# A graph layer on one core: where a sum waits for its second load of edges, and the order of two loads and two copies

## The chip, the core and the metric

The kernel runs on one core of a Trainium2 chip. The core has a matrix engine (PE, with PEld for the loading of its weights), three elementwise engines (DVE, ACT, POOL), an engine that mostly issues transfers (SP), and 16 DMA engines that carry the transfers which SP, ACT and POOL ask for. Each engine works through its own list of instructions in order and waits on semaphores for the others. The metric is the time of one execution on the device in microseconds (us); lower is better.

## The reference

A graph has 12500 nodes with 128 numbers each and 412500 edges with 48 numbers each; the edges are sorted by their target node `dst`. What is computed, cut to the core:

```python
h   = maximum(layernorm(x), 0)                     # 12500 x 128
agg = segment_sum(edge_attr_48, dst, 12500)        # 12500 x 48, the sum of a node's edges
u   = graph_globals[0]                             # the same 64 numbers for every node
hid = relu(concat([h, agg, u]) @ W1 + b1)          # 12500 x 256
out = x + hid @ W2 + b2                            # 12500 x 128
```

All numbers are fp32. `src` isn't used in the result.

## The kernel before

**Tiles.** The work goes in 12 rounds of 1024 nodes and a rest of 212. A round's nodes are two halves, A and B, of 512 (tiles `xa`, `xb`). A round has 11 groups of edges of 3072 each (576 KB), which lie in six slots (`SLOTS`): slots 0 to 3 hold two groups each, slot 4 one, slot 5 two. Each group has a load of its own: `le0.0` and `le0.1` are the first and the second load of slot 0. Eleven loads of the next round are asked for while a round runs, each as soon as the sum that read the slot is done.

**The sum of a slot.** DVE compares each edge's place with a row of 28 numbers, which gives a one-hot tile (`oh`, line 676). PE multiplies these with the edges (`add_up`, line 695): 24 products for each group, so 48 for a slot of two groups, and the first 24 read the first load alone, the last 24 the second alone. An fp32 product stands in the trace as two matmul records and two weight loads, so a slot of two groups is 96 records. The sums of the slots are called `su0` to `su5` below. They go by turns to two banks of PSUM, and ACT copies each to SBUF (`ss`, line 699), which frees the bank for the sum after the next. PE then places the sums of each group at their nodes by a second one-hot product (`place`, line 717, into `ax` and `ay`), and ACT copies these to `ags` (`sums_out`, line 760).

**The nodes.** DVE takes mean and variance of `xa` and `xb` (`stats`, line 724), ACT scales them (`norm`, line 745), PE turns them (`turn`, line 754), and the two layers follow (lines 764 and 769 into four banks, relu on ACT in line 774, line 790 for the second layer). POOL adds the bias to the old x (`xba`, `xbb`, line 749), after which ACT may ask for the next x into the same tiles.

**The order.** The class `Flow` records every operation with what it reads and writes, in the order in which `prologue`, `body` and `epilogue` are written, and works out which semaphores each must wait for. Each engine runs its operations in that order. An operation with several waits has one of them on its first instruction; the others go ahead of it as instructions of their own that only wait (`emit`, line 174; such an instruction can hold two waits). PE's loop is turned: one pass of it begins with `su3` of a round and ends with `su0`, `su1`, `su2`, the first placings and the second layer of the next one. On PE the order within a round is: `su0`, `su1`, `su2`, placings, line 790 for A and B, `su3`, `su4`, `su5`, turning of A and B, placings, lines 764 and 769.

**The lines that matter here.** Line 70 (`op`) and line 174 (`emit`): where waits are put. Line 691 (`add_up`): the operation whose waits are split. Lines 807 to 813 (`prologue`): SP's list of first loads, in which the first x stands behind slot 1's edges. Lines 924 to 933 (`body`): ACT's list at the end of a round: the copies of the turned x (line 755), the asking for the next x, the copies `ags`.

Of the kernel before, what the change touches and what calls it, by code (L numbers as in the profile page):

```python
# [20 lines left out]
T = 6  # L21
CE = P * T
CG = 4
# [3 lines left out]
IN = 1024  # L27
BN = 512
# [26 lines left out]
class Flow:  # L55
# [11 lines left out]
        self.seq = []  # L67
        self.at = None

    def op(self, eng, name, reads, writes, emit, dma=False):  # L70
        self.seq.append(dict(eng=eng, name=name, r=tuple(reads), w=tuple(writes), emit=emit, dma=dma, it=self.at))

    def chain(self, eng, name, reads, writes, *fns):

# [98 lines left out]

    def emit(self, o, waits, i):
        eng = self.of[o["eng"]]
        for s, v in waits[1:]:
            eng.wait_ge(s, v)
        made = o["emit"](i)
        if waits:
            made[0]._wait_ge(*waits[0])  # L180
        if o["name"] in self.sem:
            made[-1].then_inc(self.sem[o["name"]], self.unit(o["name"]))

# [2 lines left out]

    def straight(self, some):
        for o in some:
            self.emit(o, [(self.sem[d["name"]], self.value(d)) for d in o["waits"]], o["it"])

    def run(self):


        lo, hi = self.loop
        nc = self.nc
        start = [o for o in self.seq if o["it"] is None or o["it"] < lo]
        body = [o for o in self.seq if o["it"] == lo]
        end = [o for o in self.seq if o["it"] is not None and o["it"] > hi]
        for e in self.of:
            self.prepare(e)  # L200
        self.straight([o for o in start if o["eng"] != "PE"])
        regs = {}
        for o in body:
            for n, back in self.body.get(o["name"], []):
                u = self.unit(n)
                key = (o["eng"], u, (self.at_lo[n] - lo - back + self.extra[n]) * u)
                if key not in regs:
                    r = self.of[o["eng"]].alloc_register(f"w_{o['eng']}_{len(regs)}")
                    self.of[o["eng"]].reg_mov(r, key[2] + lo * u)
                    regs[key] = r  # L210

        def ahead(e):
            for n, c in sorted(self.ahead[e].items()):
                self.of[e].wait_ge(self.sem[n], (self.rank[n, c] + self.extra[n]) * self.unit(n))

        def repeat(o, i):
            waits = []
            for n, back in self.body.get(o["name"], []):
                u = self.unit(n)
                waits.append((self.sem[n], regs[(o["eng"], u, (self.at_lo[n] - lo - back + self.extra[n]) * u)]))  # L220
            self.emit(o, waits, i)

        def count(e):
            for (f, u, _), r in regs.items():
                if e == f:
                    self.of[e].reg_add(r, r, u)

        others = [e for e in self.of if e != "PE"]
        for e in others:
            ahead(e)  # L230
        every = {o["name"] for o in self.seq if o["it"] == hi}
        with nc.Fori(lo, hi + 1, 1, engines=[self.of[e].engine for e in others]) as i:
            for e in others:
                mine = [o for o in body if o["eng"] == e]
                for always, some in groupby(mine, lambda o: o["name"] in every):
                    with ExitStack() as last:
                        if not always:
                            last.enter_context(self.of[e].If(i < hi))
                        for o in some:
                            repeat(o, i)  # L240
            for e in others:
                count(e)
        own = [o for o in body if o["eng"] == "PE"]
        cut = [o["name"] for o in own].index(self.mark)
        with nc.Fori(0, hi - lo + 2, 1, engines=[nc.tensor.engine]) as j:
            with nc.tensor.If(j > 0):
                for o in own[cut:]:
                    repeat(o, None)
                count("PE")
            with nc.tensor.If(j < 1):  # L250
                self.straight([o for o in start if o["eng"] == "PE"])
                ahead("PE")
            with nc.tensor.If(j < hi - lo + 1):
                for brief, some in groupby(own[:cut], lambda o: o["name"] in self.brief):
                    some = list(some)
                    if not brief:
                        for o in some:
                            repeat(o, None)
                        continue
                    with nc.tensor.If(j < 1):  # L260
                        for o in some:
                            repeat(dict(o, emit=self.brief[o["name"]]), None)
                    with nc.tensor.If(j > 0):
                        for o in some:
                            repeat(o, None)
        self.straight(end)
# [151 lines left out]
def kernel(  # L418
# [18 lines left out]
    NIT = E // IE  # L437
# [61 lines left out]
    u = const.tile([G, 1], F32)  # L499
# [23 lines left out]
    f = Flow(nc, tc)  # L523
    op = f.op
    A, B, Z = 0, 1, 2
# [37 lines left out]
    def rows_of(ap, i, a, m, r):  # L563
        return span(ap, i, a, m * r).rearrange("(p r) d -> p (r d)", r=r)

    def load_x(k, a, m=P, eng="ACT"):
        r = RR[k]
        dv = xt[k].rearrange("p r d -> p (r d)")
        q = m - m % 16
        dma(eng, f"lx{k}", [], [f"x{k}"], dv[:q], lambda i: rows_of(x, i, a, q, r))  # L570
        if q < m:
            dma(eng, f"lx{k}t", [], [f"x{k}t"], dv[q:m], lambda i: rows_of(x, i, lambda i: a(i) + q * r, m - q, r))
# [118 lines left out]
    def add_up(name, k, o, ev, sv, reads, n):  # L691

        m = -(-n // CG)
        op("PE", f"su{name}", [f"oh{name}"] + reads, [f"S{k}"], lambda i: [
            nc.tensor.matmul(  # L695
                S[k][NV * c:NV * c + V, j * DE:(j + 1) * DE], o[:, (j * CG + c) * T + t], ev[:, j * CG + c, t * DE:(t + 1) * DE],
                start=(t == 0), stop=(t == T - 1), skip_group_check=True)
            for j in range(m) for t in range(T) for c in range(min(CG, n - j * CG))])
        op("ACT", f"ss{name}", [f"S{k}"], [f"ss{name}"], lambda i: [nc.scalar.copy(sv.rearrange("p j d -> p (j d)"), S[k][:, :m * DE])])  # L699

    def sums(s):
        m = len(SLOTS[s])
        add_up(s, s % 2, oh[s], e[s], ss[s], [f"e{s}.{j}" for j in range(m)], m * CG)
# [53 lines left out]
    def sums_out(k, m=P):  # L757
        h, r = HI * (k % 2), RR[k]
        op("ACT", f"ag{k}", [f"bk{k % 2}"], [f"ag{k}"], lambda i: [
            nc.scalar.copy(ag[k // 2][h:h + DE, :, :m], agg[k % 2][h:h + DE, :m * r].rearrange("p (c r) -> p r c", r=r))])  # L760
# [41 lines left out]
    def prologue():  # L802
# [2 lines left out]
            load_dst(b)  # L805
        dma("SP", "le5.1", [], ["e5.1"], e[5][:, CG:], edge_attr[:GE].rearrange("(c p t) d -> p c (t d)", p=P, t=T))
        for s in range(NS):
            if s == 2:
                load_x(A, lambda i: 0, eng="SP")
                load_x(B, lambda i: BN, eng="SP")  # L810
            for k in (0, 1):
                if (s, k) != (5, 1) and k < len(SLOTS[s]):
                    load_e(s, 1, k)
# [71 lines left out]
    def body(it):  # L885
        f.at = it

        def add_slots(*some):
            for s in some:
                sums(s)  # L890
                if it < NIT - 1:
                    load_e(s, 1)

        keep = lambda i: (i + NIT - 2) % (NIT - 1)
        farthest()
        fetch(1)
        add_slots(0, 1)
        for k in (A, B):
            stats(k)
            variance(k)  # L900
        add_slots(2)
        onehots(0)
        shift(A)
        shift(B)
        onehots(1)
        onehots(2)
        norm(A)
        norm(B)
        place(5, (0,), 0)
        place(0, (1,))  # L910
        place(1)
        places(5)
        fetch_off(1)
        places(0)
        places(1)
        for k in (A, B):
            second(k, P, ph[k], f"PH{k}", keep)
        for k in (A, B):
            add_b(k)

        add_slots(3, 4, 5)
        for s in (3, 4, 5):
            onehots(s)
        turn(A)
        turn(B, P, po, "PO")
        if it < NIT - 1:
            load_x(A, lambda i: (i + 1) % NIT * IN)
            load_x(B, lambda i: (i + 1) % NIT * IN + BN)
        for s in (2, 3, 4):
            place(s)  # L930
        place(5, (), 1)
        sums_out(A)
        sums_out(B)
        for s in (2, 3, 4):
            places(s)
        layers(layer_x)
        layers(layer_e)
        layers(relu)
# [91 lines left out]
```

## Time and profile before

| what | value |
|---|---|
| time, median of 3 runs (lowest, highest) | 268.95 us (268.59, 269.54) |
| the profiled execution's own time | 268.61 us |
| its span in the profile | 266.8 us |
| PE busy, share of the span | 246.5 us, 92% |
| DVE busy | 240.3 us, 90% |
| ACT busy | 126.3 us, 47% |
| POOL busy | 54.3 us, 20% |
| moved by DMA, mean rate | 94.33 MB, 354 GB/s |

A share of the span is a mean over a first round, which starts from nothing, eleven rounds that follow it, and a rest. The view of waits tells which engine stood still and for whom; the chain of work that ended last tells which engine set the end at each moment; the timeline gives single groups of instructions with their start (us from the span's start), their length and the idle time ahead of them. A matmul's end is modelled: a row's length holds the last record's own length, about 0.2 us, besides the steps from record to record.

### The profile page before, as it was taken

How to read it: one execution, taken by the hardware profiler on the slowest of the kernel's cores; microseconds unless marked ns; L12 is line 12 of the kernel's file. 1: busy time of each engine (PE TensorE's matmuls, PEld its weight loads, DVE VectorE, ACT ScalarE, POOL GpSimd, SP SyncE). 2: the span in 40 equal slices, each digit the busy share in tenths (PEclk: the TensorE clock that was granted, in tenths of full speed). 3: DMA queues.
4: the chain of work that ended last, by engine and by line, in shares of the span. 5: the costliest groups of instructions: out<-in, count | busy, mean ns of one | idle time of the engine just before them, and what ended most of it. 6: DMA issues, size and time to landing. Idle time of an engine off the chain costs nothing.

```text
span 266.8 us, 17173 instructions
## 1 busy us (share of the span) xinstructions
PE 246.5 (92%) x7539; PEld 191.9 (72%) x7540; DVE 240.3 (90%) x593; ACT 126.3 (47%) x314; POOL 54.3 (20%) x47
## 2 busy tenths in 40 slices
PE   0874899999999999999999999999999999999990
PEld 0864766967958949949859769679589498598580
DVE  6699999999999999989999989989899999899441
ACT  4630526545537438246445455364374373464420
POOL 8100050050140410500500501403204105007000
PEclk9975799999999999999999999999999999999999
DMA  6999999999999999999999999999999999979911
GB/s 201 289 385 383 364 391 392 390 393 390 390 393 387 390 393 371 390 392 344 391 385 350 391 345 372 393 357 378 393 343 389 394 334 390 393 232 379 377 68 63
DMA packets 79012, 94.33 MB, mean 354 GB/s; under 512 B 3227, under 2 KB 72189, under 8 KB 78998
## 3 DMA queue, kind: packets, MB, share of 16 engines
q1 hardware_dynamic: 75398, 87.63, 93.1%
q10 hardware_dynamic: 3312, 6.03, 5.9%
q0 software_dynamic: 288, 0.49, 0.7%
q8 instruction: 7, 0.11, 0.2%
q14 instruction: 7, 0.06, 0.1%
HBM read 87.75 MB, written 6.40 MB: 353 GB/s over the span
## 4 chain that ended last, share of the span: by engine, by line
PE 86%; DVE 6%; issue 2%; DMA 1%; ACT 1%; SPq 0%; DVEq 0%
PE s L695 26%; PE ph L790 17%; PE ph L764 9%; PE ax L717 7%; PE ph L769 5%; PE pt L764 4%; PE po L764 4%; PE pt L769 4%; PE ay L717 3%; DVE oh L676 3%; PE pt L754 3%; PE po L754 2%; DMA holda<-in_dst_dram 1%; DVE pl L682 1%; PE s L952 1%
## 5 line engine op out<-in xcount | busy, mean ns | idle before, releaser
L676 DVE TENSOR_TENSOR oh<-iota_v,rel_i 128x1344 f32<-128x1344 f32 (+1 forms) x78 | 130.7, 1715 | 0.0
L695 PEld LDWEIGHTS s<-e,oh 128*28 128x28 f32 x6336 | 74.7, 109 | 17.6 <-issue 14.8
L695 PE MATMUL s<-e,oh 128*28 128x48 f32 x6336 | 79.4, 210 | 6.6 <-issue 3.2
L749 POOL TENSOR_TENSOR xba<-xa,b_sb 128x512 f32<-128x512 f32 x12 | 15.5, 1288 | 191.0 <-DVE holda L794 191.0
L699 ACT COPY ss<-s 128x96 f32<-128x96 f32 (+1 forms) x72 | 16.8, 235 | 60.0 <-PE s L695 60.0
L682 DVE TENSOR_SCALAR pl<-iota_w,off_i 128x186 f32<-128x186 f32 x141 | 35.0, 307 | 0.5
L749 POOL TENSOR_TENSOR xbb<-xb,b_sb 128x512 f32<-128x512 f32 x12 | 31.1, 2592 | 0.0
L717 PE MATMUL ax<-pl,ss 128*48 128x186 f32 (+3 forms) x172 | 26.9, 298 | 0.0
L717 PE MATMUL ay<-pl,ss 128*48 128x186 f32 (+3 forms) x168 | 26.1, 296 | 0.0
L774 ACT ACTIVATE hida<-ph,bias 128x512 f32<-128x512 f32 x12 | 8.2, 687 | 35.1 <-PE ph L769 35.1
L790 PE MATMUL ph<-w,hida 128*128 128x128 f32 x192 | 24.6, 281 | 0.0
L790 PEld LDWEIGHTS ph<-w,hida 128*128 128x128 f32 x192 | 22.3, 191 | 3.2 <-issue 3.1
L790 PE MATMUL ph<-w,hidb 128*128 128x128 f32 x192 | 23.4, 275 | 0.0
L790 PEld LDWEIGHTS ph<-w,hidb 128*128 128x128 f32 x192 | 22.4, 192 | 0.0
L745 ACT ACTIVATE xna<-xa,sha,sca 128x128 f32<-128x128 f32 x48 | 19.8, 483 | 3.8 <-DVE sha L741 3.6
L717 PEld LDWEIGHTS ax<-pl,ss 128*48 128x48 f32 x172 | 17.6, 126 | 4.3 <-issue 2.0
L745 ACT ACTIVATE xnb<-xb,shb,scb 128x128 f32<-128x128 f32 x48 | 19.6, 480 | 0.0
L717 PEld LDWEIGHTS ay<-pl,ss 128*48 128x48 f32 x168 | 17.8, 124 | 0.0
L769 PE MATMUL ph<-ags,w1a 48*128 48x512 f32 x48 | 14.1, 641 | 0.0
L724 DVE BATCH_NORM_STATS2 sta<-xa 128x6 f32<-128x128 f32 x48 | 10.4, 280 | 3.8 <-DMA xa<-in_x_dram 3.7
L760 ACT COPY ags<-ax 48x512 f32<-48x512 f32 x12 | 7.0, 579 | 14.3 <-POOL xbb L749 13.4
L764 PE MATMUL ph<-hta,w1h 128*128 128x512 f32 x24 | 13.5, 645 | 0.0
(155 smaller groups left out, 305.8 us busy)
## 6 DMA issues: line engine op xcount, KB each, us to landing
e<-in_edge_attr_dram SPq DMA_DIRECT2D x133, 576.0 KB, 8.6
xa<-in_x_dram ACTq DMA_DIRECT2D x11, 256.0 KB, 5.4
xb<-in_x_dram ACTq DMA_DIRECT2D x11, 256.0 KB, 5.6
out_dram<-holda SPq DMA_DIRECT2D x11, 256.0 KB, 3.5
out_dram<-holdb SPq DMA_DIRECT2D x11, 256.0 KB, 3.5
holda<-in_dst_dram SPq DMA_DIRECT2D x4, 384.0 KB, 5.1
e<-in_edge_attr_dram SPq DMA_DIRECT2D x1, 720.0 KB, 4.3
xa<-in_x_dram SPq DMA_DIRECT2D x1, 256.0 KB, 10.0
```

Source lines behind the costliest of these rows:

```text
L676: op("DVE", f"oh{name}", reads + ["iota_v"], [f"oh{name}"], lambda i: [nc.vector.tensor_tensor(ov, iota_v[:, None, None, :].to_broadcast([ ...
L682: nc.vector.tensor_scalar(out[:, j], iota_w, o[j], None, OP.is_equal) for j in range(len(o))])
L695: nc.tensor.matmul(S[k][NV * c:NV * c + V, j * DE:(j + 1) * DE], o[:, (j * CG + c) * T + t], ev[:, j * CG + c, t * DE:(t + 1) * DE], start ...
L699: op("ACT", f"ss{name}", [f"S{k}"], [f"ss{name}"], lambda i: [nc.scalar.copy(sv.rearrange("p j d -> p (j d)"), S[k][:, :m * DE])])
L717: out.append(nc.tensor.matmul(agg[bk][h:h + DE, at:at + w], sv[:, j], pv[:, j, frm:frm + w], start=bk in fresh and bk not in seen, stop=Tr ...
L724: op("DVE", f"st{k}", [f"x{k}", f"x{k}t"], [f"st{k}"], lambda i: [nc.vector.bn_stats(st[k][:m, r], xt[k][:m, r]) for r in range(RR[k])])
L745: nc.scalar.activation(xn[k][:m, r], xt[k][:m, r], AF.Relu, bias=sh[k][:m, r:r + 1], scale=sc[k][:m, r:r + 1]) for r in range(RR[k])])
L749: nc.gpsimd.tensor_tensor(xb[k][:m], xt[k][:m], b2_sb[:m, None, :].to_broadcast([m, RR[k], D]), OP.add)])
L754: op("PE", f"tu{k}", [f"xn{k}", "ident"], [key], lambda i: [nc.tensor.transpose(pv[:, r, :m], xn[k][:m, r], ident[:m, :m]) for r in range( ...
L764: nc.tensor.matmul(o, w1h[:, a * P:(a + 1) * P], hT[k][:, :, :m], start=first, stop=False, skip_group_check=True)])
L769: nc.tensor.matmul(o, w1a[h:h + DE, a * P:(a + 1) * P], ag[k // 2][h:h + DE, :, :m], start=False, stop=True, skip_group_check=True)])
L790: nc.tensor.matmul(ov[:m, r], hid[k][:, a, r, :m], w2[:, a], start=(a == 0), stop=(a == NH - 1)) for r in range(RR[k]) for a in range(NH)])
```

## The change

It has three parts. First, an operation can name waits that are `late`: such a wait is taken from those ahead of the operation and put on a later instruction of it. `add_up` does so with the second load of a slot: its wait stands on product number 24, the first that reads this load. Second, the first x is asked for behind slot 2's edges and no longer ahead of them. Third, in each round ACT copies the two `ags` ahead of asking for the next x and no longer behind it.

```diff
-    def op(self, eng, name, reads, writes, emit, dma=False):
+    def op(self, eng, name, reads, writes, emit, dma=False, late=None):
...
     def emit(self, o, waits, i):
         eng = self.of[o["eng"]]
+        late = [(o["late"][n], s, v) for n, s, v in waits if n in o["late"]]
+        waits = [(s, v) for n, s, v in waits if n not in o["late"]]
         for s, v in waits[1:]:
             eng.wait_ge(s, v)
         made = o["emit"](i)
         if waits:
             made[0]._wait_ge(*waits[0])
+        for k, s, v in late:
+            made[k]._wait_ge(s, v)
...
-            for j in range(m) for t in range(T) for c in range(min(CG, n - j * CG))])
+            for j in range(m) for t in range(T) for c in range(min(CG, n - j * CG))], late={f"le{name}.1": CG * T})
...
         for s in range(NS):
-            if s == 2:
+            if s == 3:
                 load_x(A, lambda i: 0, eng="SP")
                 load_x(B, lambda i: BN, eng="SP")
...
         turn(A)
         turn(B, P, po, "PO")
-        if it < NIT - 1:
-            load_x(A, lambda i: (i + 1) % NIT * IN)
-            load_x(B, lambda i: (i + 1) % NIT * IN + BN)
         for s in (2, 3, 4):
             place(s)
         place(5, (), 1)
         sums_out(A)
         sums_out(B)
+        if it < NIT - 1:
+            load_x(A, lambda i: (i + 1) % NIT * IN)
+            load_x(B, lambda i: (i + 1) % NIT * IN + BN)
```

On PE, the sums `su0` to `su2` of a round stood like this before, with all the semaphores that each first product and the waiting instructions ahead of it wait for (`le` are loads of edges, `oh` one-hot tiles, `ss` copies that free the bank):

```order
L695 MATMUL s_65<-e_74,oh_87 28x48 [waits le0_0,le0_1,oh0]
L695 MATMUL s_65<-e_74,oh_87 28x48 x47
L695 MATMUL s_66<-e_75,oh_88 28x48 [waits le1_1,le1_0,ss5,oh1]
L695 MATMUL s_66<-e_75,oh_88 28x48 x47
L695 MATMUL s_65<-e_76,oh_89 28x48 [waits le2_1,le2_0,oh2,ss0]
L695 MATMUL s_65<-e_76,oh_89 28x48 x47
```

In the changed kernel PE has at the same place (line numbers are four higher):

```order
L699 MATMUL s_65<-e_74,oh_87 28x48 [waits le0_0,oh0]
L699 MATMUL s_65<-e_74,oh_87 28x48 x23
L699 MATMUL s_65<-e_74,oh_87 28x48 [waits le0_1]
L699 MATMUL s_65<-e_74,oh_87 28x48 x23
L699 MATMUL s_66<-e_75,oh_88 28x48 [waits le1_0,ss5,oh1]
L699 MATMUL s_66<-e_75,oh_88 28x48 x23
L699 MATMUL s_66<-e_75,oh_88 28x48 [waits le1_1]
L699 MATMUL s_66<-e_75,oh_88 28x48 x23
L699 MATMUL s_65<-e_76,oh_89 28x48 [waits le2_0,oh2,ss0]
L699 MATMUL s_65<-e_76,oh_89 28x48 x23
L699 MATMUL s_65<-e_76,oh_89 28x48 [waits le2_1]
L699 MATMUL s_65<-e_76,oh_89 28x48 x23
```

Each of the three has one wait less at its first product and one on its 25th. At the starts of `su1` and `su2` four waits became three, which takes away one of the two instructions that only wait.

The sums `su3` to `su5`, which follow one another on PE later in the round, stood like this before:

```order
L695 MATMUL s_66<-e_77,oh_90 28x48 [waits le3_0,le3_1,oh3]
L695 MATMUL s_66<-e_77,oh_90 28x48 x47
L695 MATMUL s_65<-e_78,oh_91 28x48 [waits le4_0,ss2]
L695 MATMUL s_65<-e_78,oh_91 28x48 x23
L695 MATMUL s_66<-e_79,oh_92 28x48 [waits le5_0,le5_1,ss3]
L695 MATMUL s_66<-e_79,oh_92 28x48 x47
```

In the changed kernel the first products of `su3` and `su5` wait for `le3_0,oh3` and `le5_0,ss3`, and their 25th products for `le3_1` and `le5_1`; `su4`, which has one load, is as it was. So five products of a round carry a wait in the midst of a sum.

On ACT, the end of a round stood like this before, from the copies of the turned x to the first relu:

```order
L755 COPY hta<-pt 128x512 [waits tu0]
L755 COPY htb<-po 128x512 [waits tu1]
L238 COMPARE_AND_BRANCH
L530 ISA
L530 DMA xa<-in_x_dram 128x512 [waits xb0]
L530 ISA
L530 DMA xb<-in_x_dram 128x512 [waits xb1]
L236 UNCONDITIONAL_BRANCH
L760 COPY ags<-ax 48x512 [waits pc4]
L760 COPY ags<-ay 48x512 [waits pc5_1]
L774 ACTIVATE hida<-ph_70,bias 128x512 [waits ha0_0]
```

In the changed kernel ACT has there:

```order
L759 COPY hta<-pt 128x512 [waits tu0]
L759 COPY htb<-po 128x512 [waits tu1]
L764 COPY ags<-ax 48x512 [waits pc4]
L764 COPY ags<-ay 48x512 [waits pc5_1]
L242 COMPARE_AND_BRANCH
L534 ISA
L534 DMA xa<-in_x_dram 128x512 [waits xb0]
L534 ISA
L534 DMA xb<-in_x_dram 128x512 [waits xb1]
L240 UNCONDITIONAL_BRANCH
L778 ACTIVATE hida<-ph_70,bias 128x512 [waits ha0_0]
```

The two copies no longer stand behind the waits for POOL (`xb0`, `xb1`), and the two loads stand behind two more copies and the waits for PE's placings (`pc4`, `pc5_1`).

More of the change, by code (lines that the diff above doesn't have):

```diff
@@ L68, in __init__ @@
         self.at = None
-    def op(self, eng, name, reads, writes, emit, dma=False):
-        self.seq.append(dict(eng=eng, name=name, r=tuple(reads), w=tuple(writes), emit=emit, dma=dma, it=self.at))
+    def op(self, eng, name, reads, writes, emit, dma=False, late=None):
+        self.seq.append(dict(eng=eng, name=name, r=tuple(reads), w=tuple(writes), emit=emit, dma=dma, it=self.at, late=late or {}))
     def chain(self, eng, name, reads, writes, *fns):
@@ L188, in straight @@
         for o in some:
-            self.emit(o, [(self.sem[d["name"]], self.value(d)) for d in o["waits"]], o["it"])
+            self.emit(o, [(d["name"], self.sem[d["name"]], self.value(d)) for d in o["waits"]], o["it"])
     def run(self):
@@ L219, in repeat @@
                 u = self.unit(n)
-                waits.append((self.sem[n], regs[(o["eng"], u, (self.at_lo[n] - lo - back + self.extra[n]) * u)]))
+                waits.append((n, self.sem[n], regs[(o["eng"], u, (self.at_lo[n] - lo - back + self.extra[n]) * u)]))
             self.emit(o, waits, i)
```

## The prediction

> **What bounds the kernel now.** I read the page first, then the chain that ended last in order of time, then PE's waits.
>
> ```profile
> span 266.8 us, 17173 instructions
> PE 246.5 (92%) x7539; PEld 191.9 (72%) x7540; DVE 240.3 (90%) x593; ACT 126.3 (47%) x314; POOL 54.3 (20%) x47
> ...
> 47.88 3.77 PE ph L790 x32
> ...
> 217.50 3.77 PE ph L790 x32
> ...
> 236.34 3.77 PE ph L790 x32
> ```
>
> The three rows of the chain are the second layer in rounds 1, 10 and 11 (counted from 0). Rounds 10 and 11 lie 18.84 us apart, and so do rounds 1 to 10 in the mean: (217.50 - 47.88) / 9 = 18.85. So from round 1 on a round is 18.84 us whatever DMA and DVE do. These are all of PE's waits in the whole run:
>
> ```profile
> PE s L603 <- issue: 7.4, 1, 7.4
> PE s L695 <- issue: 3.2, 2, 1.8
> PE s L695 <- DMA e<-in_edge_attr_dram: 2.6, 2, 1.7
> PE s L695 <- ACT ss L699: 0.7, 1, 0.7
> ```
>
> Every one lies before 34 us. PE waits for edges twice, 2.6 us in all, in the first round; behind that, never. So rounds 1 to 11 are PE's own list, and only what makes this list shorter helps there; a wait moved to a later product is a wait that is already over.
>
> The first round is another matter. PE, DVE and the clock in it, by stretches of 4 us (busy time of PE, PEld, DVE, ACT, POOL, then clock, DMA share, GB/s), with round 1 for comparison:
>
> ```profile
> 16.00:20.00 4.00, 2.24 (x96) 1.98 (x96) 3.93 (x14) 0.00 (x0) 0.00 (x0) 0.57 1.08 393
> ...
> 24.00:28.00 4.00, 1.51 (x65) 1.35 (x69) 3.81 (x21) 0.30 (x1) 0.00 (x0) 0.50 1.08 385
> 28.00:32.00 4.00, 4.00 (x141) 3.52 (x134) 3.86 (x10) 2.29 (x7) 0.00 (x0) 0.72 1.09 352
> ...
> 48.00:66.70 18.70, 18.70 (x613) 14.37 (x612) 18.29 (x47) 9.59 (x24) 3.83 (x2) 1.00 1.08 391
> ```
>
> DVE is the full one there, PE is half idle and at half clock. What DVE's list ends in:
>
> ```profile
> 30.24 1.65 ACT L745 ACTIVATE xna<-xa,sha,sca 128x128 f32<-128x128 f32 x4 [0.98 <-DVE sha L741]
> 31.80 1.63 ACT L745 ACTIVATE xnb<-xb,shb,scb 128x128 f32<-128x128 f32 x4
> 33.34 0.31 ACT L699 COPY ss<-s 128x96 f32<-128x96 f32 x2
> ...
> 33.60 1.22 PE L695 MATMUL s<-e,oh 128*28 128x48 f32 x96 [0.70 <-ACT ss L699]
> ```
>
> ACT scales x when DVE has the variance (30.2 us), and only behind both halves copies the sum su3, whose bank su5 needs. So su5 of round 0 starts at 33.60 by DVE and ACT, and PE was ready 0.70 us before.
>
> **Part 1, the late wait, round 0.** It lets su0, su1, su2 start on one load. It can win PE some of the 2.6 us of waits, and all of it goes into the wait for ACT at 33.60, which grows from 0.70. DVE's list has no wait for these sums' ends that binds. Worth on the path: 0.
>
> **Part 1, rounds 1 to 11.** Here the wait itself costs nothing, but the instructions that only wait do. The joins between sums, by two groups of the page (mean ns of one record is the 109 and the 210) and three rows of the timeline (96 records are one sum of 48 products, 288 are su0 to su2, 240 are su3, su4, su5):
>
> ```profile
> L695 PEld LDWEIGHTS s<-e,oh 128*28 128x28 f32 x6336 | 74.7, 109 | 17.6 <-issue 14.8
> L695 PE MATMUL s<-e,oh 128*28 128x48 f32 x6336 | 79.4, 210 | 6.6 <-issue 3.2
> ...
> 212.92 1.22 PE L695 MATMUL s<-e,oh 128*28 128x48 f32 x96
> ...
> 212.92 3.49 PE L695 MATMUL s<-e,oh 128*28 128x48 f32 x288
> ...
> 202.36 2.81 PE L695 MATMUL s<-e,oh 128*28 128x48 f32 x240
> ```
>
> One sum: 1.22 less the last record's own 0.21 is 1.01 us for 95 steps, 10.6 ns each. Three sums: 3.49 - 1.22 = 2.27 us for 192 more records, of which 192 x 10.6 ns = 2.04 are plain; 0.23 is left for two joins. The second group: 2.81 - 1.22 = 1.59 for 144 more, 1.53 plain; 0.06 is left for its two joins. The same products, banks and copies, but su1 and su2 wait for four semaphores each, su4 for two, su5 for three. I take this as the price of the waits: none for two, 0.03 to 0.06 for three, 0.11 to 0.12 for four.
>
> After the change su1 and su2 wait for three, su5 for two. The first group's joins go from 0.23 to twice 0.03 to 0.06, a gain of 0.11 to 0.17; su5's join gains 0.03 to 0.06. I take 0.13 and 0.03, so **0.16 us a round, 11 rounds, 1.8 us**. At most all of it goes, 0.23 + 0.06 = 0.29 a round, 3.2 us. su0 and su3 lose a wait too, but no row parts it from what else lies at their starts: 0 to 0.03 each, I take 0.
>
> Against it stand five waits a round within sums, and the trace has none such. Nearest: su4 and su5 have a wait on their first product, and their joins cost 0.06 for two, at most 0.03 each: 0 to 0.15 a round. Far end: such a product's weights can't be loaded early, 0.109 each, 0.55 a round. I take 0, since su4's kind of join is nearest and shows nothing.
>
> **Part 2, x behind slot 2.** SP's asking, its time to landing (10.0 us) and DVE's reading in round 0, from timeline and DMA view:
>
> ```profile
> 10.59 3.06 SPq L530 DMA_DIRECT2D xa<-in_x_dram  x1
> ...
> xa<-in_x_dram SPq DMA_DIRECT2D x1, 256.0 KB, 10.0
> ...
> 25.46 0.86 DVE L724 BATCH_NORM_STATS2 sta<-xa 128x6 f32<-128x128 f32 x4
> ```
>
> xa landed at 10.6 + 10.0 = 20.6 and was read at 25.46, when DVE's list came to it. It now stands behind two loads of 576 KB, at 385 GB/s 1.5 us each: it lands at 23.7, 1.8 us early still; xb follows it within about 1 us and is read 1.4 us later. Cost 0; without this cover each us late would move su5 by one. Edges of slot 2 land earlier, for which see part 1: 0.
>
> **Part 3, the copies of sums, round 0.** Rows of the timeline from round 0, a late round and the last one:
>
> ```profile
> 40.11 0.58 ACT L760 COPY ags<-ax 48x512 f32<-48x512 f32 x1 [3.59 <-POOL xbb L749]
> ...
> 34.76 0.65 PE L754 MATMUL pt<-ident,xna 128*128 128x128 f32 x4
> 43.26 3.53 PE L695 MATMUL s<-e,oh 128*28 128x48 f32 x288
> ...
> 205.10 0.66 PE L754 MATMUL pt<-ident,xna 128*128 128x128 f32 x4
> ...
> 242.77 0.66 PE L754 MATMUL pt<-ident,xna 128*128 128x128 f32 x4
> 248.68 1.13 PE L769 MATMUL ph<-ags,w1a 48*128 48x512 f32 x4
> ...
> 245.44 0.58 ACT L760 COPY ags<-ay 48x512 f32<-48x512 f32 x1
> ```
>
> ACT's copies stood 3.59 us behind the asking for xb, which waits for POOL. From the turning to the next su0 PE took 43.26 - 34.76 = 8.50 us; in a later round 212.92 - 205.10 = 7.82. The 0.68 between is PE waiting for `ags`. The last round asks for no x and shows the new order: there the second copy ends 245.44 + 0.58 - 242.77 = 3.25 us behind the turning, and its reader starts 5.91 behind it. So **0.68 us goes, once**; later rounds have it already.
>
> **Part 3, the asking, later rounds.** ACT's asking for xa and DVE's first statistics in a late round, those of round 1, and the time to landing:
>
> ```profile
> 206.50 0.34 ACTq L530 DMA_DIRECT2D xa<-in_x_dram  x1
> ...
> 211.81 0.87 DVE L724 BATCH_NORM_STATS2 sta<-xa 128x6 f32<-128x128 f32 x4
> ...
> 43.70 0.87 DVE L724 BATCH_NORM_STATS2 sta<-xa 128x6 f32<-128x128 f32 x4
> ...
> xa<-in_x_dram ACTq DMA_DIRECT2D x11, 256.0 KB, 5.4
> ```
>
> xa was asked for 206.50 - 205.10 = 1.4 us behind the turning. Behind both copies it is about 2.9 (the second starts 2.67 behind it in the last round, and ACT asked 0.2 us into the copy ahead). So x comes 1.5 us later, and DVE was waiting for it: 206.50 + 5.4 is 211.9, and it starts at 211.81. Cover: DVE then started 217.50 - 211.81 = 5.7 us ahead of PE's second layer, and will start 4.2 ahead. In round 1 it was 47.88 - 43.70 = 4.2 as well, and that round was 18.84 long with no wait of PE. DVE's work is 18.29 in 18.70 us, under the new round of 18.68. Cost 0; behind DVE stand ACT's scaling and POOL, and if they came later than in round 1 PE would wait for the copy of su3, as in round 0.
>
> **Sum.** -0.68 - 1.8 = -2.5 us. On the profiled execution's 268.61 that is 266.1; the median shown stands 0.34 above it, so **266.4**. With the ends of the joins and the inner waits: 268.95 - 0.68 - 3.2 = 265.1 to 268.95 - 0.68 = 268.3.
>
> **Rivals.** *The joins don't pay for waits.* PE may read ahead of what it executes, so that waits already over cost nothing, and the joins differ for another cause, say when the copies come. Then only 0.68 goes: 268.3. Against it: the two groups share everything but their waits. [...]
>
> *Slower: a wait within a sum stops the loading of weights ahead.* At each 25th product the weights are loaded only when the product's turn comes, 0.109 us by the row above. Five a round are 0.55, less the 0.16 gained, over 11 rounds +4.2, less 0.68: 272.5. It decides from 0.044 us a wait on, (0.16 + 0.06) / 5. For it: no such wait is in the trace. Against it: first products with a wait of their own show at most 0.03.
>
> *x comes too late.* If transfers of x took 1.5 us more than the 5.4, PE would wait for what round 1 just allows: a shift, paid about once, 1 us: 267.4.
>
> *The clock.* PE finishes its first sums earlier in round 0, waits longer for 33.60, and starts su5 at the 0.50 of the stretch 24 to 28. The stretches show it at half for some 12 us in one piece; a quarter of that, 3 us, at half speed costs 1.5, and I take 1.7: 268.1. Against it: PE's first sums also stand still at 1.8 and 1.4 us of "issue", which no load shortens, so they hardly finish earlier. [...]
>
> **Numbers.** Forecast 0.59, joins don't pay 0.16, slower 0.10, clock 0.08, late x 0.07. A measurement tells about 0.3%, 0.8 us, from no change. Faster by more: forecast, late x and half of the clock's case, 0.70; within: 0.20; slower: 0.10. The range goes from all joins gone, 265.1, to past the cases at 268.1 and 268.3: 268.5; it leaves out the slow case and some of the edges.
>
> **What would show it.** Right: rounds of 18.68 us between second layers in the chain; three sums in a row in about 3.36 us and su3 to su5 in 2.78; `ags` in round 0 no longer behind POOL; su5 of round 0 at 33.6; DVE's first statistics about 4.2 us ahead of the second layer. Wrong: rounds of 18.84 (joins), sums of 96 records longer than 1.22 (inner waits), waits of PE for `ss` in later rounds (x), a clock of 0.5 behind 32 us.

## The result, and the profile after

| what | before | after |
|---|---|---|
| time, median of 8 runs each, side by side (lowest, highest) | 268.92 us (268.58, 269.54) | 266.07 us (265.02, 267.49) |
| the profiled execution's own time | 268.61 us | 265.81 us |
| its span | 266.8 us | 264.1 us |

The ratio of after to before is 0.9895, with an interval of 0.9867 to 0.9923: 2.85 us less. The forecast was 266.4, 2.5 us less, in a range of 265.1 to 268.5.

The head of the page of the changed kernel:

```profile
span 264.1 us, 17149 instructions
...
PE 243.5 (92%) x7539; PEld 189.3 (72%) x7540; DVE 240.4 (91%) x593; ACT 126.7 (48%) x314; POOL 54.1 (20%) x47
```

PE runs the same 7539 matmul records and is busy 3.0 us less. Its profile holds 24 instructions fewer (17149 for 17173), two a round: the ones that `su1` and `su2` lost. Where the time went is read in the chain that ended last (start, length, what ran):

```profile
47.45 3.77 PE ph L794 x32
...
215.03 3.77 PE ph L794 x32
...
233.65 3.77 PE ph L794 x32
```

These are the same three second layers as before. A round is now 233.65 - 215.03 = 18.62 us, and (215.03 - 47.45) / 9 = 18.62 in the mean; it was 18.84. From round 1 to round 11 PE needs 233.65 - 47.45 = 186.20 us where it needed 236.34 - 47.88 = 188.46: **2.26 us less, in ten equal steps.** Ahead of round 1's second layer only 0.43 is gained.

What became shorter within a round, in PE's timeline of a late round:

```profile
200.11 2.81 PE L699 MATMUL s<-e,oh 128*28 128x48 f32 x240
202.84 0.66 PE L758 MATMUL pt<-ident,xna 128*128 128x128 f32 x4
...
210.67 3.27 PE L699 MATMUL s<-e,oh 128*28 128x48 f32 x288
```

The second group (240 records) takes 2.81 us as before, and from the turning to the first sum it is 7.83, before 7.82. Only the first group is shorter, 3.27 for 3.49. Of its 3.27 - 1.22 = 2.05 us for two more sums, 2.04 are plain steps, so its two joins now cost 0.01 where they cost 0.23. The round's whole gain of 0.22 is there.

Round 0, first PE, then ACT, in the timeline:

```profile
26.98 1.11 PE L699 MATMUL s<-e,oh 128*28 128x48 f32 x66 [3.32 <-issue]
...
30.99 4.34 PE L699 MATMUL s<-e,oh 128*28 128x48 f32 x240
35.27 0.66 PE L758 MATMUL pt<-ident,xna 128*128 128x128 f32 x4
...
43.09 3.27 PE L699 MATMUL s<-e,oh 128*28 128x48 f32 x288
```

```profile
37.33 0.58 ACT L764 COPY ags<-ax 48x512 f32<-48x512 f32 x1 [0.30 <-PE ay L721]
37.94 0.58 ACT L764 COPY ags<-ay 48x512 f32<-48x512 f32 x1
```

The copies `ags` wait 0.30 for PE's placing and no longer 3.59 for POOL; the turning to the next first sum takes 43.09 - 35.27 = 7.82 us, before 8.50: 0.68 gone. But the turning comes at 35.27 and not at 34.76, 0.51 later: `su3` to `su5` take 4.34 us where a later round takes 2.81. The stretches of 4 us with the clock (the number behind POOL's) say why:

```profile
24.00:28.00 4.00, 1.02 (x66) 0.91 (x66) 3.78 (x22) 0.30 (x1) 0.00 (x0) 0.93 1.08 384
28.00:32.00 4.00, 4.00 (x70) 3.37 (x72) 3.90 (x9) 2.32 (x7) 0.00 (x0) 0.50 1.09 355
32.00:36.00 4.00, 4.00 (x209) 3.93 (x200) 3.93 (x10) 1.92 (x8) 0.34 (x1) 0.69 1.08 390
```

Before, the clock was 0.72 and 1.00 in the last two. So up to round 1's second layer: -0.68 for the copies, -0.22 for the first joins, +0.51 for the clock, together -0.39 of the measured -0.43.

All of PE's waits after:

```profile
PE s L607 <- DVE fc L597: 7.3, 1, 7.3
PE s L699 <- issue: 6.4, 2, 3.3
PE s L699 <- DMA e<-in_edge_attr_dram: 0.4, 1, 0.4
```

The waits for edges fell from 2.6 to 0.4 us, and "issue" rose from 3.2 to 6.4. What PE no longer spent on waiting for edges it spent on "issue"; two of the runs below show the same exchange without any late wait.

### The profile page after: what moved, and what is told of

It is laid out like the page before. It is cut to its first block, busy times and chain, and to the rows that moved or that the text cites. A ratio compares the mean times of both kernels' runs of the same rounds, so it can differ in the third digit from the quotient of the medians.

```text
span 264.1 us, 17149 instructions
## 1 busy us (share of the span) xinstructions
PE 243.5 (92%) x7539; PEld 189.3 (72%) x7540; DVE 240.4 (91%) x593; ACT 126.7 (48%) x314; POOL 54.1 (20%) x47
## 4 chain that ended last, share of the span: by engine, by line
PE 89%; DMA 4%; issue 3%; SPq 2%; DVE 0%
PE s L699 28%; PE ph L794 17%; PE ph L768 9%; PE ax L721 8%; PE ph L773 5%; DMA e<-in_edge_attr_dram 4%; PE pt L768 4%; PE po L768 4%; PE pt L773 4%; PE ay L721 3%; PE pt L758 3%; PE po L758 2%; SPq L534 2%; PE s L956 1%; PE ph L997 0%
## 5 line engine op out<-in xcount | busy, mean ns | idle before, releaser
L699 PEld LDWEIGHTS s<-e,oh 128*28 128x28 f32 x6336 | 72.8, 109 | 17.1 <-issue 15.1
L699 PE MATMUL s<-e,oh 128*28 128x48 f32 x6336 | 76.7, 210 | 6.9 <-issue 6.4
L794 PE MATMUL ph<-w,hida 128*128 128x128 f32 x192 | 24.6, 281 | 0.0
L773 PE MATMUL ph<-ags,w1a 48*128 48x512 f32 x48 | 13.5, 641 | 0.0
L768 PE MATMUL pt<-hta,w1h 128*128 128x512 f32 x24 | 12.3, 592 | 0.0
```

The lines of the kernel that those rows point to most:

```text
L699: nc.tensor.matmul(S[k][NV * c:NV * c + V, j * DE:(j + 1) * DE], o[:, (j * CG + c) * T + t], ev[:, j * CG + c, t * DE:(t + 1) * DE], start ...
L768: nc.tensor.matmul(o, w1h[:, a * P:(a + 1) * P], hT[k][:, :, :m], start=first, stop=False, skip_group_check=True)])
L773: nc.tensor.matmul(o, w1a[h:h + DE, a * P:(a + 1) * P], ag[k // 2][h:h + DE, :, :m], start=False, stop=True, skip_group_check=True)])
L794: nc.tensor.matmul(ov[:m, r], hid[k][:, a, r, :m], w2[:, a], start=(a == 0), stop=(a == NH - 1)) for r in range(RR[k]) for a in range(NH)])
```

## The experiments

Twelve runs were made in three groups, each beside runs of the kernel before on the same chip (medians 268.76, 268.92 and 268.97 us). Diffs are against the changed kernel unless said otherwise.

### The parts alone

**The late wait alone** (part 1; the other two parts put back):

```diff
-            if s == 3:
+            if s == 2:
...
+        if it < NIT - 1:
+            load_x(A, lambda i: (i + 1) % NIT * IN)
+            load_x(B, lambda i: (i + 1) % NIT * IN + BN)
         for s in (2, 3, 4):
...
         sums_out(B)
-        if it < NIT - 1:
-            load_x(A, lambda i: (i + 1) % NIT * IN)
-            load_x(B, lambda i: (i + 1) % NIT * IN + BN)
```

> Part 1 alone: the late waits, with x asked for where it was in both places. Theory: the joins ahead of su1 and su2 get shorter because one of two instructions that only wait goes, 0.22 us a round in the changed kernel's trace, so rounds of 18.62 us and about 268.95 - 11 x 0.22 = 266.5 us; in round 0 the 0.68 us of waiting for ags stays. Rival, it is the earlier copies that shorten the rounds: rounds of 18.84 and 268.9 us.

Measured: 266.10 us, ratio 0.9907 (0.9885 to 0.9929). Its chain and ACT's row in round 0:

```profile
215.24 3.77 PE ph L794 x32
...
233.85 3.77 PE ph L794 x32
```

```profile
40.13 0.58 ACT L764 COPY ags<-ax 48x512 f32<-48x512 f32 x1 [3.51 <-POOL xbb L753]
```

Rounds of 18.61 us (18.62 in the changed kernel) come from part 1 alone. The wait of `ags` for POOL in round 0 stays, so it is part 3's.

**The copies alone** (part 3; against the kernel before):

```diff
-        if it < NIT - 1:
-            load_x(A, lambda i: (i + 1) % NIT * IN)
-            load_x(B, lambda i: (i + 1) % NIT * IN + BN)
         for s in (2, 3, 4):
...
         sums_out(B)
+        if it < NIT - 1:
+            load_x(A, lambda i: (i + 1) % NIT * IN)
+            load_x(B, lambda i: (i + 1) % NIT * IN + BN)
```

> Part 3 alone: ags copied ahead of the asking for x. Theory: rounds stay at 18.84 us, the 0.68 us wait for ags in round 0 goes, 268.95 - 0.7 = 268.25 us; DVE's statistics in late rounds start 4.2 us ahead of the second layer in place of 5.7. Rival, the later asking makes DVE late and PE wait: longer rounds, over 269 us.

Measured: 267.97 us, ratio 0.9969 (0.9946 to 0.9991). Its chain, PE's timeline in round 0, and the stretches:

```profile
218.31 3.77 PE ph L790 x32
...
237.15 3.77 PE ph L790 x32
```

```profile
31.60 4.82 PE L695 MATMUL s<-e,oh 128*28 128x48 f32 x240
36.35 0.66 PE L754 MATMUL pt<-ident,xna 128*128 128x128 f32 x4
...
44.17 3.51 PE L695 MATMUL s<-e,oh 128*28 128x48 f32 x288
```

```profile
28.00:32.00 4.00, 4.00 (x68) 3.25 (x64) 3.86 (x10) 2.26 (x7) 0.00 (x0) 0.50 1.09 358
32.00:36.00 4.00, 4.00 (x213) 4.00 (x208) 3.93 (x10) 1.85 (x6) 0.21 (x1) 0.50 1.08 385
```

Rounds stay at 18.84. From the turning to the next sum it is 44.17 - 36.35 = 7.82 us, so part 3 takes the 0.68 as it does in the changed kernel; the median fell by 0.8. This execution (269.30 us, 1.3 above the median of its kernel) shows round 0 at half clock, with the turning at 36.35, **without any late wait**: the low clock there isn't made by part 1. PE's waits for sums in it:

```profile
PE s L695 <- issue: 5.5, 2, 3.3
PE s L695 <- DMA e<-in_edge_attr_dram: 1.1, 2, 0.8
```

Up to the turning this kernel has the lists of the one before, which had 3.2 and 2.6 us. So the exchange of waits for edges against "issue" doesn't come from part 1 either.

**The first x alone** (part 2; against the kernel before):

```diff
-            if s == 2:
+            if s == 3:
```

> Part 2 alone (the first x behind slot 2's edges), the rest as before. Theory 'part 2 is worth nothing': rounds of 18.84 us, first x landed about 24.6 us and read at about 25.3 to 26 us without a wait of DVE, time as before, 268.9 within 0.4. Rival 'part 2 costs' (the tendency of the two pairs with and without it, 0.3 and 0.8 us): 269.3 to 269.7, and the cost is in round 0, as more time at half clock while su3 to su5 run. Rival 'part 2 gains': slot 2's earlier edges bring the first turning forward, under 34.8 us, and the time to 268.4 or less.

Measured: 268.93 us beside 268.97, ratio 1.0005 (0.9984 to 1.0025). In its timeline the last sum of round 0 stands where it stood, again behind ACT:

```profile
33.55 1.22 PE L695 MATMUL s<-e,oh 128*28 128x48 f32 x96 [0.88 <-ACT ss L699]
```

Part 2 alone is worth nothing that can be measured. PE's waits show the exchange here as well:

```profile
PE s L695 <- issue: 5.9, 2, 3.4
PE s L695 <- DMA e<-in_edge_attr_dram: 0.2, 1, 0.2
```

**Parts 1 and 3 without part 2**, run three times, and the changed kernel twice more:

```diff
-            if s == 3:
+            if s == 2:
```

Without part 2, first run, with a forecast on the low clock in round 0 of the changed kernel (0.50 and 0.69 in the two stretches from 28 to 36 us):

> Parts 1 and 3, the first x back ahead of slot 2's edges. [...] With slot 2's edges later this should happen less: su5 of round 0 at 33.6, the turning at 34.8 in place of 35.3, a narrower spread than the changed kernel's 265.0 to 267.5, median about 268.95 - 0.7 - 2.4 = 265.8 or below. Rival, the place of the first x does nothing: the same spread and 266.1 us.

The second pair, without part 2 and with it:

> Parts 1 and 3 without part 2, on the same chip as the changed kernel. [...]

> The changed kernel itself beside the next one on the same chip: 266.1 us, with a spread over 2 us from the clock in round 0.

The third pair:

> Parts 1 and 3 without part 2, third time, beside the changed kernel on this chip. Theory 'part 2 is worth nothing': 266.1 within 0.4 of the changed kernel's median. Rival 'part 2 costs': about 265.7, 0.4 to 0.8 below it.

> The changed kernel once more, to stand beside the same kernel without part 2 on this chip. Theory 'part 2 is worth nothing': both medians within 0.4 us of one another, about 266.1. Rival 'part 2 costs': this one 0.4 to 0.8 us above the other, for the third time.

Measured without part 2: 265.79, 265.66 and 265.81 us. With it: 266.07 (the result), 266.46 and 265.21. In the second pair it was 0.80 slower with part 2, in the third 0.60 faster, which is more than the 0.4 that was expected of no effect, and the other way round than a cost. All runs together have medians of 265.73 us (18 without) and 265.81 (19 with). So the lead that the first two pairs seemed to show didn't hold, and these runs show no difference between the two.

**How much cover x has.** The first x behind slot 3's edges too:

```diff
-            if s == 3:
+            if s == 4:
```

> The changed kernel, but the first x is asked for behind slot 3's edges, so two more loads of 576 KB stand ahead of it. It should land some 3 us later, at about 27.6 us instead of 24.6; DVE wants it at about 25.3 to 26. Theory 'x has 0.7 us of cover after the change and each us beyond moves su5 of round 0': DVE waits about 2 us, the first turning moves from 35.3 to about 37, and the time is about 268.2, with rounds of 18.62. Rival 'PE's first pass is bound by its own instructions, not by x': DVE waits but the first turning stays at 34.9 to 36.1, time 266.0 to 266.5. If part 2 costs by a low clock, that grows too.

Measured: 266.71 us, ratio 0.9928 (0.9909 to 0.9948), where the changed kernel in the same group had 0.9868 (0.9846 to 0.9889): 1.5 us above it, and 0.9 above the one without part 2. SP, the DMA view, DVE and PE in round 0:

```profile
17.88 1.41 SPq L534 DMA_DIRECT2D xa<-in_x_dram  x1
```

```profile
xa<-in_x_dram SPq DMA_DIRECT2D x1, 256.0 KB, 8.4
```

```profile
26.30 0.87 DVE L728 BATCH_NORM_STATS2 sta<-xa 128x6 f32<-128x128 f32 x4 [1.00 <-DMA xa<-in_x_dram]
```

```profile
34.46 1.22 PE L699 MATMUL s<-e,oh 128*28 128x48 f32 x96 [0.58 <-ACT ss L703]
35.62 0.66 PE L758 MATMUL pt<-ident,xna 128*128 128x128 f32 x4
```

By the records x landed at 17.88 + 8.4 = 26.3 us, 1.7 later than in the changed kernel and not the 3 expected; DVE waited 1.00 us for it and `su5` started at 34.46, behind ACT. So the cover is real and short: one place further in SP's list it is gone. What the wait costs is less clear. Neither the 268.2 us nor the turning at 37 that were expected came; the turning lies where the rival put it (34.9 to 36.1), the time a little above the rival's 266.0 to 266.5. Between the two profiled executions the turning is 0.35 later (35.62 for 35.27) and the time 0.37 longer (266.18 for 265.81). The 1.5 us between the medians may be in part the clock: the five executions of the changed kernel in this group had a mean granted clock of 0.974 to 0.985, four of the six here 0.960 to 0.972.

### What a wait costs

**Late waits for `su1` and `su2` only**, with parts 2 and 3 put back as in the first experiment:

```diff
-... late={f"le{name}.1": CG * T})
+... late={f"le{name}.1": CG * T} if name in (1, 2) else {})
```

> Part 1 for su1 and su2 alone, nothing else changed. Theory (a second wait-only instruction ahead of a sum costs about 0.1 us, one costs nothing): all of part 1's gain is here, rounds of 18.62 us, 266.5 us. Rival (each semaphore costs, as the prediction took it: 0.03 to 0.06 for the third, so su5 and its kind gain too): rounds of 18.65 to 18.7 us, with the rest of the gain in su0, su3 and su5.

Measured: 266.77 us, ratio 0.9918 (0.9897 to 0.9939). Two second layers in its chain, and round 0:

```profile
197.81 3.77 PE ph L794 x32
...
216.43 3.77 PE ph L794 x32
```

```profile
31.87 4.85 PE L699 MATMUL s<-e,oh 128*28 128x48 f32 x240
36.65 0.66 PE L758 MATMUL pt<-ident,xna 128*128 128x128 f32 x4
```

Rounds of 18.62: the whole gain of a round comes from the two joins that lost an instruction. `su0`, `su3` and `su5`, which also lost a semaphore but kept the one instruction that only waits, are worth nothing. Round 0 ran long in this execution (4.85 us for `su3` to `su5`, the turning at 36.65), at the half clock that is told of below and that also comes without late waits. The median stands 0.67 above that of part 1 whole (266.10), and the clock differs between the two as well: at 0.979 and above both take 265.9 to 266.3 us, at 0.960 to 0.961 both take 266.8 to 267.3.

**More instructions that only wait.** The changed kernel, with waits that are already over repeated ahead of four sums (`su1` then has two such instructions, `su2` three, `su4` two, `su5` one that holds two waits):

```diff
-        for s, v in waits[1:]:
+        again = {"su1": 1, "su2": 3, "su4": 2, "su5": 1}.get(o["name"], 0)
+        for s, v in waits[1:] + waits[-1:] * again:
             eng.wait_ge(s, v)
```

> The changed kernel with waits that are over written again ahead of some sums, on the same semaphores: ahead of su1 two instructions that only wait in place of one, ahead of su2 three, ahead of su4 two, ahead of su5 one that holds two waits in place of one wait. Theory (instructions cost, semaphores don't; the first is hidden): the steps into su1 and su4 grow by about 0.095 us each, into su2 by 0.15 to 0.2, into su5 by 0; rounds of 18.62 + 0.35 to 0.4 = about 19.0 us and some 270.2 us. Rival (distinct semaphores or late landings cost): nothing grows, 266 us. Rival (a property of su1 and su2 alone): su4's step stays at 22 ns.

Measured: 270.88 us, ratio 1.0064 (1.0044 to 1.0084), 4.4 above the changed kernel on that chip (266.46). Its profile has 17197 instructions, 48 more than the changed kernel's, so four a round: none came for `su5`'s second wait. Chain and timeline:

```profile
218.69 3.77 PE ph L795 x32
...
237.69 3.77 PE ph L795 x32
```

```profile
222.38 2.87 PE L700 MATMUL s<-e,oh 128*28 128x48 f32 x240
...
233.01 3.60 PE L700 MATMUL s<-e,oh 128*28 128x48 f32 x288
```

A round is 237.69 - 218.69 = 19.00 us, 0.38 more. The first group has three instructions more and takes 3.60 for 3.27, **0.11 us for each**; the second has one more that counts (`su4`'s second) and takes 2.87 for 2.81. Read from record to record (medians of the later rounds), the step into `su1` is 122 ns with two such instructions and 23 with one, that into `su2` 216 ns with three, 110 with two (before) and 16 with one; that into `su4` 120 ns with two and 22 with one; the step into `su5`, whose single instruction holds two waits here, is no longer than the 47 ns that it was (at most 30, which takes back a part of `su4`'s). So the price is not one of semaphores: one instruction that only waits costs next to nothing, and each further one about 0.1 us. The steps of 16 to 47 ns with one have to be held against plain steps at the same place. Plain steps are 10.6 ns in the mean but come in fours (22 or 23, 7, 6, 7 ns, or 16, 13, 8, 6), and a join falls on the first of a four: the 23, 16 and 22 ns into `su1`, `su2` and `su4` are plain steps, and only `su5`'s 47 stand above one, by some 30 ns.

**More waits within sums.** Every product from the 25th on carries the wait, 120 a round instead of 5:

```diff
-            made[k]._wait_ge(s, v)
+            for n in range(k, len(made)):
+                made[n]._wait_ge(s, v)
```

> The changed kernel with the late wait on each of the last 24 products of a sum, 120 waits within sums a round in place of 5. Theory (a wait within a sum that is over is free): rounds of 18.62 us, 266.1 us. Rival (such a wait stops the loading of weights ahead, up to 0.109 us each): 115 more waits at 0.109 would be up to 12.5 us a round; already 0.005 us each would show as rounds of 19.2 us.

Measured: 265.73 us, ratio 0.9879 (0.9853 to 0.9904). PE's timeline:

```profile
219.62 2.81 PE L700 MATMUL s<-e,oh 128*28 128x48 f32 x240
...
230.18 3.27 PE L700 MATMUL s<-e,oh 128*28 128x48 f32 x288
```

The same 2.81 and 3.27 us. So waits that the products carry themselves, and that are over, cost nothing here, 5 or 120 a round.

## Why the prediction was right, point by point

**The bound** was right: rounds 1 to 11 are PE's list, and what left this list is what the time lost, in ten equal steps.

**Part 1, later rounds: right mechanism, its size too small.** The term "0.13 and 0.03, so 0.16 us a round, 11 rounds, 1.8 us" measured 0.22 a round, 2.5 us. The step that was off is the price list: "none for two, 0.03 to 0.06 for three, 0.11 to 0.12 for four" counted semaphores. What is paid is the second instruction that only waits. With four waits an operation has two of them (its first product carries one wait, an instruction holds two), with three or two it has one; the 24 instructions fewer, two a round, are these. So three waits cost no more than two: `su1` and `su2` gained all of their 0.11 each, and `su5`, which went from three to two, gained nothing: the second group's 0.06 is still there. The run with late waits for `su1` and `su2` only has the same round. So of the signs, rounds of 18.68 us and three sums in 3.36 came out lower (18.62 and 3.27), and the shorter 2.78 for `su3` to `su5` didn't come (2.81).

**The inner waits** cost nothing, as taken: in late rounds the step into the 25th product of these sums is 22 to 24 ns without the wait and 22 to 23 with it. With 120 a round they still cost nothing, so the rival of 272.5 is out by experiment. **"The joins don't pay for waits"** is out too: added instructions gave back 4.4 us.

**Part 1, round 0** was taken at 0, and it came out at 0, by another way than the one named. The prediction sent the 2.6 us of saved waits into the wait for ACT; the profile has them in "issue" (3.2 to 6.4), ahead of that point. And the late wait isn't what moved them: the copies alone have 1.1 us of waits for edges and 5.5 of "issue", the first x alone 0.2 and 5.9. The last 66 records of `su2` start at 26.98 here, the last 67 at 27.34 before. With the copies alone they start at 27.04, and with late waits for two sums at 27.32. So this point doesn't follow the waits for loads; its place in PE's list stands in the last section. That `su5` starts at 33.6 was a sign of being right and didn't come: in this execution it starts at 33.87, without a wait for ACT, behind sums at a low clock.

**Part 2** was taken at 0 and is 0. Its cover was taken as 1.8 us, x landing at 23.7. The DMA view, SP's row and DVE's:

```profile
xa<-in_x_dram SPq DMA_DIRECT2D x1, 256.0 KB, 8.8
```

```profile
15.78 1.44 SPq L534 DMA_DIRECT2D xa<-in_x_dram  x1
```

```profile
25.31 0.87 DVE L728 BATCH_NORM_STATS2 sta<-xa 128x6 f32<-128x128 f32 x4
```

It landed at 15.78 + 8.8 = 24.6, so 0.7 us were to spare. The loads that it was put behind were counted at their transfer time of 1.5 us each; SP came to ask for x 5.2 us later than before (10.59), and it then landed 1.2 us sooner after the asking. The answer held by less than half the margin that was claimed, and one place further DVE waits, as the run behind slot 3's edges shows.

**Part 3, round 0**: 0.68 forecast, 8.50 - 7.82 = 0.68 measured. **The asking for x**: ACT's row and DVE's in a late round,

```profile
205.50 0.34 ACTq L534 DMA_DIRECT2D xa<-in_x_dram  x1
```

```profile
210.75 0.87 DVE L728 BATCH_NORM_STATS2 sta<-xa 128x6 f32<-128x128 f32 x4 [0.29 <-DMA xa<-in_x_dram]
```

are 205.50 - 202.84 = 2.7 us behind the turning (2.9 forecast) and 215.03 - 210.75 = 4.3 ahead of the second layer (4.2 forecast). PE never waited for it.

**The clock** was a rival with 0.08 and a price of 1.7 us. In the profiled execution a part of it did happen, 0.51, and hid the part of the joins that was underestimated: -0.68 - 2.5 + 0.5 is -2.7 us, the change of the span. So two misses of opposite sign, 0.7 us too little for the joins and 0.5 of clock taken at nothing, lie behind a forecast that is only 0.3 us off: that closeness is in part luck; where the gain came from was foreseen. The sign "a clock of 0.5 behind 32 us" came in part, 0.69 there in the profiled execution. The same low clock stands in the run of the copies alone, and the runs of the late wait alone and of parts 1 and 3 had 1.00 behind 32 us: a late wait is neither needed for it nor enough. Whether it makes it more frequent, these single executions can't say.

## What to carry to other kernels

On an engine that is the bound, count the instructions that only wait ahead of each operation, not the semaphores: here one cost at most some 30 ns (`su5`'s step of 47), and each further one 0.11 us. Waits put on later products, which are there anyway, cost nothing here: with 5 and with 120 a round the two groups took 2.81 and 3.27 us. Ahead of moving a load back in a queue, take the margin from when the queue will ask for it (5.2 us later here), and not from the transfer times of what stands ahead alone (twice 1.5 us); and don't read a lead of 0.3% from two pairs of medians without the granted clock of each execution beside them.

## What the runs showed of the hardware

**The first instruction that only waits was nearly free, the second wasn't**, although the 96 records ahead of it keep PE busy for 1.0 us: the step into the next sum is 16 to 47 ns with one, 110 to 122 with two, 216 with three. Two that follow one another start 0.11 us apart in the trace (235.17 and 235.28 us ahead of `su2` in the run with more of them), which is the price of one. Why the first costs so little and the second 0.11 us remains open.

**The clock in round 0 differs from execution to execution**, with the same or nearly the same work. Granted clock of two stretches, and the start of round 0's turning:

| kernel | 28 to 32 us | 32 to 36 us | turning |
|---|---|---|---|
| before | 0.72 | 1.00 | 34.76 |
| first x alone | 0.75 | 1.00 | 34.71 |
| parts 1 and 3 (first run) | 0.67 | 1.00 | 34.87 |
| changed kernel (result) | 0.50 | 0.69 | 35.27 |
| part 1 alone | 0.73 | 1.00 | 34.85 |
| changed kernel (second) | 0.58 | 0.57 | 36.05 |
| changed kernel (third) | 0.59 | 1.00 | 35.38 |
| copies alone | 0.50 | 0.50 | 36.35 |
| late waits for two sums | 0.50 | 0.50 | 36.65 |

Nearly 2 us lie between them, two thirds of the whole change. In the second and the third execution of the changed kernel PE's first work also began 0.7 us later (8.0 for 7.3 us), which is in their turnings too. The mean granted clock, which stands on record for each execution, goes with the time: of the 19 executions of the changed kernel, the eleven at 0.974 or above took 264.91 to 265.91 us, the five at 0.967 to 0.973 took 266.33 to 266.70, the three at 0.960 to 0.961 took 267.13 to 267.49. So medians of five or six of them can differ by over a us between groups (265.21 and 266.46). The clock doesn't follow PE's busy row: with the copies alone PE is busy 4.00 of 4.00 us in both stretches, and the clock stands at 0.50 in both; in the kernel before PE is busy 3.30 us in the second, at a clock of 1.00. A busy row of PE is modelled. What sets the clock these runs don't show.

**The first pass of PE's list stands still for "issue" twice, at fixed places of the list.** In the chain of the changed kernel:

```profile
17.65 3.11 issue
20.76 2.90 PE s L699 x127
23.66 3.32 issue
26.98 1.11 PE s L699 x66
```

Over all fourteen kept traces PE goes on at 20.4 to 21.6 and at 26.6 to 27.8 us. The rounds behind it, which run the same instructions again, don't show it. The places can be counted in the records. The kernel before passes 126 records between the two points, the changed kernel 127; with their weight loads and the four or two instructions that only wait these are 252 + 4 and 254 + 2, **256 instructions in both**, as in every other trace (257 with more waits added). And a packet of 16 KB starts on a DMA queue that the profile calls "instruction" 2.2 to 2.6 us ahead of each point in every trace (in the changed kernel at 18.30 and 24.50), though the points themselves move by 1.2 us between traces; between 33 and 246 us no such packet is moved. One more, at 29.71 in the changed kernel, goes by without a standstill. No run changed these packets or the length of the list between the points by itself, so what holds PE there isn't shown.
